# A mixture-of-experts kernel in which the last possible blocks of tokens stand behind a branch on the number of blocks needed

## The chip, the cores and the metric

The kernel runs on one core of a Trainium2 chip. A core has five engines with a queue of instructions each: TensorE (PE, matrix products; its weight loads are listed as PEld), VectorE (DVE), ScalarE (ACT), GpSimd (POOL) and SyncE (SP), and DMA engines that move data between the main memory (HBM) and the core's own memory (SBUF). TensorE writes into banks of a small accumulation memory, from which VectorE and ScalarE read. Engines wait for each other by semaphores. The metric is the time of one execution on the device in microseconds, as a median of several runs.

## The reference

The input is 2048 tokens of 256 numbers. A causal attention with 16 heads is added to it and the sum normed. Then comes the part that the change touches, a mixture of 16 experts of which each token uses two:

```
scores = softmax(t @ gate_w.T);  weights, indices = top_k(scores, 2)
for e in range(16):
    w_e = sum(where(indices == e, weights, 0), axis=-1)
    y = y + swiglu(t, w1[e], w3[e], w2[e]) * w_e[:, None]     # inner width 176
z = swiglu(t, sw1, sw3, sw2)                                  # shared experts, width 352
return layernorm(x + y + z)
```

Here swiglu(t, a, b, o) is (silu(t @ a.T) * (t @ b.T)) @ o.T. Each expert is applied only to the tokens that chose it, which the kernel has to sort out itself.

## The kernel before

**Attention** takes the first part, to about 600 us of the profiled execution. Near its end the gate is computed for each quarter of 512 tokens (`choose`, `settle`), and `scatter` writes each token's row (256 numbers, its number and its first expert) with an indirect DMA into `xg` in HBM, twice, once for each of its two experts. Every expert has room for 2048 rows there; unused rows hold a blank row whose number lies outside the result.

**Blocks.** An expert's rows are worked off in blocks of 128 rows. 4096 rows in all, spread over 16 experts with a partly filled block each, need 47 blocks at most (NBLK = (4096 - 16) // 128 + 16). `table` works out on VectorE, from the experts' counts, the running sum `end` of the experts' blocks, and from it the starting row (`row`) and the expert (`own`) of each block. Blocks beyond the number needed get the blank rows behind the last expert. `keys` gives each block a number by which its rows know whether this is their first or second expert.

**The pipeline of a block b** uses all five engines:
- `load_block`: SP reads `row[b]` into a register and loads 128 rows (129 KB) from `xg` into `xb`. Eight buffers exist, and eight loads (DEPTH + 2) are issued ahead.
- `turn`: TensorE transposes the block (`px`), VectorE copies it to SBUF (`xbT`).
- `hidden`: TensorE reads `own[b]` into a register and multiplies with this expert's w1 and w3 (`ph`); ScalarE takes the Silu (`ru`), VectorE multiplies (`rh`).
- `turn_hidden`: TensorE transposes that (`pT`), ScalarE copies it (`hT`).
- `output`: TensorE multiplies with w2 (`py`), ScalarE copies the result (`yb`), VectorE works out where each row goes (`to`), and GpSimd scatters the rows with an indirect DMA into `yg` in HBM. Rows with a place beyond 4095 are not written.

TensorE's instructions stay in the order in which they are written down: hidden(b), output(b - 1), turn_hidden(b), turn(b + 2). The other engines' orders are made by a scheduler. Banks, `yb`, `to` and `xbT` come from small rings of two or three buffers, so that a step waits until an earlier block has left its buffer.

**Shared experts and the end.** The shared experts' products go through `shared_hidden(c, i)` (`h` on TensorE, `u` on ScalarE, `sh` on VectorE) and `shared_out(c)` (`pz` on TensorE, `z` on VectorE). Those of quarters 3 and 0 and one piece of quarter 1 stand ahead of the blocks; the rest of quarter 1 and quarter 2 stand behind. Then `fetch` loads the two results of each token from `yg` (`got`, eight loads of 512 KB; the first waits until every scatter into `yg` has landed), and `combine` weights and adds them to `z` (VectorE), takes mean and variance (`st`, `m`), a root (`rs`, ScalarE with its own table load) and writes the normed rows `o`, which SP stores.

Of the kernel before, what the change touches and what calls it, by code (L numbers as in the profile page):

```python
# [11 lines left out]
I32 = mybir.dt.int32  # L12
# [5 lines left out]
P = 128  # L18
# [9 lines left out]
NEXP, INTER, SHARED = 16, 176, 352  # L28
# [8 lines left out]
NBLK = (2 * S - NEXP) // P + NEXP  # L37
WARM = 3
LAST = 2
DEPTH = 6  # L40
SCALE = 0.25
EPS = 1e-5
# [4 lines left out]
def block_kernel(  # L47
# [14 lines left out]
    nc = tc.nc  # L62
# [78 lines left out]
    def matmul(*args, **kw):  # L141
        pe(nc.tensor.matmul, *args, **kw)

    def transpose(*args):
        pe(nc.tensor.transpose, *args)
# [31 lines left out]
    def turned(c, bank):  # L177
        for k in range(2):
            pt = bank(f"pt1_{c}_{k}")
            for t in range(4):  # L180
                transpose(pt[:, t * P : (t + 1) * P], xr[c][:, t, k * P : (k + 1) * P], ident)
            nc.vector.tensor_copy(x1T[c][:, k, :], pt)
# [75 lines left out]
    def disjoint(those, group, put):  # L258

        if those:  # L260
            tc.declare_no_dep(put, group=group, reason="no two go to the same rows")
        tc.add_to_no_dep_group(group, put)
        those.append(put)

    def wait_for(those, load):

        for put in those:
            tc.add_manual_dep(
                load.ins, put.name,
                mybir.DependencyInfo(mybir.DependencyClass.Sync, mybir.DependencyReason.DATA),  # L270
                reason="rows of any scatter",
            )
# [12 lines left out]
    with ExitStack() as att:  # L285
# [378 lines left out]
        at = {}  # L664
        chosen = {}

        def put(step, what, *args):
            at.setdefault(step, []).append(lambda: what(*args))
# [23 lines left out]
        for (g, c), i in s_last.items():  # L692
            put(i + (4 if g + 1 < G else 2), finish, g, c)
            if g == G - 1:
                put(i + 2, normed, c)
                if c != LAST:
                    put(i + 6, turned, c, bank)
# [42 lines left out]
    fp1 = ctx.enter_context(tc.tile_pool(name="fp1", bufs=1))  # L740
# [7 lines left out]
    for j in range(2):  # L748
# [5 lines left out]
    blocks = fp1.tile([P, 1], F32, tag="blocks", name="blocks")  # L754
    nc.gpsimd.iota(
        blocks, pattern=[[0, 1]], base=0, channel_multiplier=1,
# [53 lines left out]
    def shared(c):  # L810
        for i in range(NSC):
            shared_hidden(c, i)
        shared_out(c)

    def table():

        count = fp1.tile([P, NEXP], F32, tag="count", name="count")
        nc.vector.tensor_tensor(count, fill, room, ALU.subtract)
        whole = fp1.tile([P, NEXP], I32, tag="whole", name="whole")
        nc.vector.tensor_scalar(whole, count, float(P - 1), None, ALU.add)  # L820
        nc.vector.tensor_scalar(whole, whole, 7, None, ALU.logical_shift_right)
        nb = fp1.tile([P, NEXP], F32, tag="nb", name="nb")
        nc.vector.tensor_copy(nb, whole)
        ends = fp1.tile([P, NEXP, NEXP], F32, tag="ends", name="ends")
        nc.vector.tensor_tensor(
            ends, upto, nb.unsqueeze(1).to_broadcast([P, NEXP, NEXP]), ALU.mult
        )
        end = fp1.tile([P, NEXP], F32, tag="end", name="end")
        nc.vector.tensor_reduce(end, ends, AX.X, ALU.add)

        past = fp1.tile([P, NEXP], F32, tag="past", name="past")
        nc.vector.tensor_scalar(past, end, blocks, None, ALU.is_le)
        owner = fp1.tile([P, 1], F32, tag="owner", name="owner")
        nc.vector.tensor_reduce(owner, past, AX.X, ALU.add)
        nc.vector.tensor_tensor(past, past, nb, ALU.mult)
        first = fp1.tile([P, 1], F32, tag="first", name="first")
        nc.vector.tensor_reduce(first, past, AX.X, ALU.add)
        nc.vector.tensor_tensor(first, blocks, first, ALU.subtract)
        nc.vector.tensor_scalar(
            first, first, float(S // P - 1), float(P), ALU.min, ALU.mult  # L840
        )
        nc.vector.scalar_tensor_tensor(first, owner, float(S), first, ALU.mult, ALU.add)
        row = fp1.tile([P, 1], I32, tag="row", name="row")
        nc.vector.tensor_scalar(row, first, float(NEXP * S), None, ALU.min)
        own = fp1.tile([P, 1], I32, tag="own", name="own")
        nc.vector.tensor_scalar(own, owner, float(NEXP - 1), None, ALU.min)
        return own, row, end

    def keys(end):

# [13 lines left out]
    def load_block(b, row):  # L864
        r = nc.values_load(
            row[b : b + 1, 0:1], engines=[mybir.EngineType.SP],
            min_val=0, max_val=NEXP * S,
            skip_runtime_bounds_check_because="an expert below their number, a block of its room",
        )
        xb[b] = fp8.tile([P, ROW], F32, tag="xb", name=f"xb{b}")  # L870
        load = nc.sync.dma_start(out=xb[b], in_=xg[bass.ds(r, P), :])
        tc.keep_in_program_order(load)
        if b == 0:
            wait_for(scattered, load)

    def turn(b):
        px = ps_a.tile([P, 2, P], F32, tag="t", name=f"px{b}")
        for k in range(2):
            transpose(px[:, k, :], xb[b][:, k * P : (k + 1) * P], ident)
        xbT[b] = fp3.tile([P, 2, P], F32, tag="xbT", name=f"xbT{b}")  # L880
        nc.vector.tensor_copy(xbT[b], px)  # L881

    def hidden(b, own):
        expert[b] = nc.values_load(
            own[b : b + 1, 0:1], engines=[mybir.EngineType.PE], min_val=0, max_val=NEXP - 1,
            skip_runtime_bounds_check_because="a count of experts, held below their number",
        )
        ph = ps_a.tile([P, 2 * INTER], F32, tag="h", name=f"ph{b}")
        for k in range(2):
            matmul(  # L890
                ph, lhsT=xbT[b][:, k, :],
                rhs=w13[:, k].rearrange("p n f -> p (n f)")[
                    :, bass.ds(expert[b] * (2 * INTER), 2 * INTER)
                ],
                start=(k == 0), stop=(k == 1),
            )
        u = fp2.tile([P, INTER], F32, tag="ru", name=f"ru{b}")
        nc.scalar.activation(u, ph[:, :INTER], AF.Silu)  # L898
        us[b] = fp2.tile([P, INTER], F32, tag="rh", name=f"rh{b}")
        nc.vector.tensor_tensor(us[b], u, ph[:, INTER:], ALU.mult)  # L900

    def turn_hidden(b):
        pT = ps_a.tile([P, 2, P], F32, tag="t", name=f"pT{b}")
        for k in range(2):
            transpose(pT[:HK, k, :], us[b][:, k * HK : (k + 1) * HK], ident)
        hT[b] = fp3.tile([HK, 2, P], F32, tag="hT", name=f"hT{b}")
        nc.scalar.copy(hT[b], pT[:HK])  # L907
# [3 lines left out]
    def output(b, key):  # L911
        py = ps_a.tile([P, E], F32, tag="y", name=f"py{b}")
        for k in range(2):
            matmul(
                py, lhsT=hT[b][:, k, :],
                rhs=w2r[:, k].rearrange("p n e -> p (n e)")[:, bass.ds(expert[b] * E, E)],
                start=(k == 0), stop=(k == 1),
            )
        yb = fp3.tile([P, E], F32, tag="yb", name=f"yb{b}")
        nc.scalar.copy(yb, py)  # L920
        to = fp3.tile([P, 1], I32, tag="to", name=f"to{b}")
        nc.vector.scalar_tensor_tensor(  # L922
            to, xb[b][:, E + 1 : ROW], key[:, b : b + 1], xb[b][:, E : E + 1],
            ALU.not_equal, ALU.add,
        )
        disjoint(
            back, "back",
            nc.gpsimd.indirect_dma_start(  # L928
                out=yg[:, :], out_offset=bass.IndirectOffsetOnAxis(ap=to[:, 0:1], axis=0),
                in_=yb, in_offset=None, bounds_check=2 * S - 1, oob_is_err=False,  # L930
            ).ins,
        )
# [41 lines left out]
    shared_hidden(3, 1)  # L974
    turned(LAST, spare)
    shared_hidden(3, 2)
    both = choose(LAST, spare)
    shared_out(3)
    shared_hidden(0, 0)
    settle(LAST, spare, both)  # L980
    for t in range(4):
        scatter(LAST, t)
    own, row, end = table()
    for b in range(DEPTH + 2):
        load_block(b, row)
    key = keys(end)
# [1 line left out]
    shared_hidden(0, 2)  # L988
    shared_out(0)
    shared_hidden(1, 0)  # L990
    turn(0)
    turn(1)
    for b in range(NBLK):
        hidden(b, own)
        if b > 0:
            output(b - 1, key)
        turn_hidden(b)
        if b + 2 < NBLK:
            turn(b + 2)
        if b + DEPTH + 2 < NBLK:  # L1000
            load_block(b + DEPTH + 2, row)
    output(NBLK - 1, key)
    shared_hidden(1, 1)
    shared_hidden(1, 2)
    shared_out(1)
    shared(LAST)
    fetched = {}
# [72 lines left out]
```

## Time and profile before

| what | value |
|---|---|
| median of 3 runs | 818.64 us (816.54 to 819.76) |
| the profiled execution, its time | 821.03 us |
| the profiled execution, its span | 819.3 us |
| busy: PE, PEld, DVE, ACT, POOL | 790.6, 371.8, 552.0, 452.9, 328.0 us |
| first load of a block issued | 637.0 us |
| last product of a block on TensorE starts | 777.74 us |
| last instruction of ScalarE's normed rows starts | 814.95 us |

The span reaches from the first to the last instruction; the time of an execution also holds what lies around it. A row of the timeline gives the start in microseconds, the duration, the engine, the line, the operation with the tiles that it writes and reads, how often it stands there, and in brackets the idle time ahead of it with the engine that ended it. All matmuls have line L139, a helper's, so they are told apart by their tiles. A row of the table by stretches gives the stretch, its length, the busy time of PE, PEld, DVE, ACT and POOL with the number of their instructions, TensorE's granted clock, the DMA engines' busy share and GB/s. In the chain that ended last each row is what the next one waited for.

### The profile page before, as it was taken

The page shows a single profiled execution, that of the slowest core. Times are in us where ns is not written, and L with a number is a line of the kernel's source. Part 1 is how long each engine was busy: PE and PEld are TensorE (multiplying, and loading weights), DVE is VectorE, ACT ScalarE, POOL GpSimd, SP SyncE. Part 2 cuts the span into 40 slices and gives each one's busy share as a digit, 9 for nine tenths or more (in the row PEclk, how much of TensorE's full clock was granted, in tenths as well). Part 3 has the DMA queues.
Part 4 walks back from the last instruction along what each step waited for, and adds up shares of the span by engine and source line. Part 5 has one row for each costly group of instructions (what it writes and reads, how often), then busy time and mean ns, then how long its engine had stood idle before and what let it go on. Part 6 is the DMA issues. An engine that isn't in the chain of part 4 may idle for free. (4 is left out here: it accounts for less than half of the span.)

```text
span 819.3 us, 15191 instructions
## 1 busy us (share of the span) xinstructions
PE 790.6 (96%) x5146; PEld 371.8 (45%) x5146; DVE 552.0 (67%) x1503; ACT 452.9 (55%) x1014; POOL 328.0 (40%) x562
## 2 busy tenths in 40 slices
PE   7999999999999999999999999999999899999994
PEld 3444433534333344534344444443356466666652
DVE  2769888986777887787887777887466233333266
ACT  1143556387776886676786668756531233333346
POOL 2042535344454554455354546433553133333300
PEclk9999999999999999999999999999899999999998
DMA  5479999960000000010000000001152322222062
GB/s 145 130 190 334 325 331 325 318 191 2 1 1 2 1 1 2 1 36 18 2 1 1 2 1 1 2 1 53 52 161 78 98 84 86 83 79 76 16 206 102
DMA packets 68339, 72.56 MB, mean 89 GB/s; under 512 B 5056, under 2 KB 62499, under 8 KB 68262
## 3 DMA queue, kind: packets, MB, share of 16 engines
q1 hardware_dynamic: 63006, 62.43, 26.3%
q0 software_dynamic: 3792, 8.43, 2.9%
q10 hardware_dynamic: 1464, 0.72, 0.4%
q8 instruction: 42, 0.69, 0.3%
q14 instruction: 35, 0.29, 0.1%
HBM read 27.10 MB, written 46.43 MB: 90 GB/s over the span
## 5 line engine op out<-in xcount | busy, mean ns | idle before, releaser
L534 ACT ACTIVATE p<-s 128x512 f32<-128x512 f32 (+3 forms) x640 | 292.7, 540 | 131.6 <-PE m L139 77.5
L139 PE MATMUL m<-k,q 32*128 32x512 f32 (+3 forms) x1280 | 303.3, 564 | 0.8 <-DVE rot L422 0.5
L139 PE MATMUL s<-qa,k 32*128 32x512 f32 (+3 forms) x1280 | 280.4, 558 | 3.3 <-DVE avs L562 2.3
L489 DVE TENSOR_REDUCE pm<-m 128x1 f32<-128x512 f32 x384 | 237.5, 681 | 44.0 <-PE m L139 43.6
L566 POOL TENSOR_TENSOR avs<-avs,more 128x512 f32<-128x512 f32 (+3 forms) x125 | 136.8, 1094 | 166.4 <-ACT more L565 162.8
L139 PEld LDWEIGHTS s<-qa,k 32*128 32x128 f32 x1280 | 107.3, 184 | 120.3 <-ACT p L534 67.4
L139 PE MATMUL av<-p,v 128*32 128x512 f32 (+3 forms) x1280 | 156.6, 546 | 0.9 <-ACT p L534 0.4
L139 PEld LDWEIGHTS m<-k,q 32*128 32x128 f32 x1280 | 122.8, 183 | 44.4 <-issue 12.0
L484 DVE CUSTOM_DVE_ANT_0 m<-m,qmask 128x512 f32<-128x512 f32 (+3 forms) x256 | 118.2, 521 | 28.8 <-PE m L139 25.8
L565 ACT COPY more<-av 128x512 f32<-128x512 f32 (+3 forms) x125 | 65.6, 525 | 38.3 <-PE av L139 31.4
L928 POOL DMA_INDIRECT yg<-yb,to x47 | 46.3, 985 | 99.1 <-DVE to L922 51.0
L538 POOL TENSOR_SCALAR_AFFINE_SELECT p<-p 128x128 f32<-128x128 f32 x256 | 70.6, 297 | 38.2 <-ACT p L534 36.4
L139 PEld LDWEIGHTS av<-p,v 128*32 128x32 f32 x1280 | 27.3, 108 | 104.5 <-ACT p L534 53.6
L139 PE MATMUL ph<-w,xbT 128*128 x188 | 68.8, 490 | 2.3 <-DVE xbT L881 1.7
L900 DVE TENSOR_TENSOR rh<-ru,ph 128x176 f32<-128x176 f32 x47 | 15.9, 337 | 61.9 <-ACT ru L898 61.9
L898 ACT ACTIVATE ru<-ph 128x176 f32<-128x176 f32 x47 | 14.9, 318 | 66.9 <-PE ph L139 65.6
L139 PE MATMUL py<-w2r,hT 88*128 x188 | 48.5, 380 | 0.5 <-ACT hT L907 0.5
L139 PE MATMUL h<-xT,cs 128*128 128x512 f32 (+1 forms) x96 | 43.3, 597 | 2.4 <-ACT u L791 1.4
L277 POOL DMA_INDIRECT xg<-xr,slot x32 | 31.1, 972 | 32.6 <-issue 21.3
L139 PEld LDWEIGHTS ph<-w,xbT 128*128 128x128 f32 x188 | 32.4, 191 | 23.2 <-issue 13.4
L139 PEld LDWEIGHTS py<-w2r,hT 88*128 88x128 f32 x188 | 35.5, 189 | 13.3 <-ACT hT L907 1.1
L427 POOL TENSOR_TENSOR k<-rot 128x512 f32<-128x512 f32 x16 | 20.3, 1268 | 42.6 <-DVE rot L425 42.6
(146 smaller groups left out, 649.0 us busy)
## 6 DMA issues: line engine op xcount, KB each, us to landing
xg<-hot SPq DMA_DIRECT2D x16, 2064.0 KB
xb<-xg SPq DMA_DIRECT2D x47, 129.0 KB
w<-in_w_dram SPq DMA_DIRECT2D x4, 1408.0 KB
got<-yg SPq DMA_DIRECT2D x8, 512.0 KB
w2r<-in_w_dram SPq DMA_DIRECT2D x2, 1408.0 KB
xr<-in_x_dram SPq DMA_DIRECT2D x4, 512.0 KB
out_dram<-o SPq DMA_DIRECT2D x8, 256.0 KB
cs<-in_rope_dram SPq DMA_DIRECT2D x16, 80.0 KB
```

Of the source, the lines that this page charges most:

```text
L139: tc.keep_in_program_order(op(*args, **kw))
L277: put = nc.gpsimd.indirect_dma_start(out=xg[:, :], out_offset=bass.IndirectOffsetOnAxis(ap=slot[:, j, i : i + 1], axis=0), in_=xr[c][:, t, ...
L427: nc.gpsimd.tensor_tensor(ks[g, c], tmp[:, 0, :], tmp[:, 1, :], ALU.add)
L484: nc.vector.tensor_tensor_reduce(out=ps[:, :n], in0=ps[:, :n], in1=qmask[:, CH - n :], scale=1.0, scalar=3.0 * NEG, op0=ALU.add, op1=ALU.m ...
L489: nc.vector.tensor_reduce(to, ps, AX.X, ALU.max)
L534: nc.scalar.activation(pr[:, n0:], ps[:, n0:], AF.Exp, scale=SCALE)
L538: nc.gpsimd.affine_select(out=diag, in_=diag, pattern=[[1, P]], base=0, channel_multiplier=-1, compare_op=ALU.is_ge, fill=0.0,)
L565: nc.scalar.copy(more[:, n0:], pv[:, n0:])
L566: nc.gpsimd.tensor_tensor(to, to, more[:, n0:], ALU.add)
L898: nc.scalar.activation(u, ph[:, :INTER], AF.Silu)
L900: nc.vector.tensor_tensor(us[b], u, ph[:, INTER:], ALU.mult)
L928: nc.gpsimd.indirect_dma_start(out=yg[:, :], out_offset=bass.IndirectOffsetOnAxis(ap=to[:, 0:1], axis=0), in_=yb, in_offset=None, bounds_c ...
```

## The change

The loop over the blocks becomes a function `in_turn(first, last)` that starts and ends its own pipeline. It is called for blocks 0 to 41. Then the number of blocks that the routing needs, the last entry of `end`, which `table` now also returns as an integer in a tile of its own, is read into a register on every engine, and a branch follows: if it is over 42 (OFTEN), the five remaining blocks are loaded and worked off by a second `in_turn`; if not, none of their instructions is executed. The shared experts and the end stand behind the branch.

```
+OFTEN = 42
 def table():
...
+        total = fp1.tile([P, 1], I32, tag="total", name="total")
+        nc.vector.tensor_copy(total, end[:, NEXP - 1 :])
-        return own, row, end
+        return own, row, end, total
...
-    turn(0)
-    turn(1)
-    for b in range(NBLK):
-        hidden(b, own)
-        if b > 0:
-            output(b - 1, key)
-        turn_hidden(b)
-        if b + 2 < NBLK:
-            turn(b + 2)
-        if b + DEPTH + 2 < NBLK:
-            load_block(b + DEPTH + 2, row)
-    output(NBLK - 1, key)
+    def in_turn(first, last):
+
+        turn(first)
+        turn(first + 1)
+        for b in range(first, last):
+            hidden(b, own)
+            if b > first:
+                output(b - 1, key)
+            turn_hidden(b)
+            if b + 2 < last:
+                turn(b + 2)
+            if b + DEPTH + 2 < last:
+                load_block(b + DEPTH + 2, row)
+        output(last - 1, key)
+
+    in_turn(0, OFTEN)
+    blocks_in_all = nc.values_load(
+        total[0:1, 0:1], min_val=0, max_val=NBLK,
+        skip_runtime_bounds_check_because="the sum of the experts' blocks, NBLK at most",
+    )
+    with tc.If(blocks_in_all > OFTEN):
+        for b in range(OFTEN, NBLK):
+            load_block(b, row)
+        in_turn(OFTEN, NBLK)
     shared_hidden(1, 1)
     shared_hidden(1, 2)
     shared_out(1)
```

More of the change, by code (lines that the diff above doesn't have):

```diff
@@ L982, in block_kernel @@
         scatter(LAST, t)
-    own, row, end = table()
+    own, row, end, total = table()
     for b in range(DEPTH + 2):
```

## The prediction, made before the result was known

> **What bounds the kernel now.** I read the busy table by stretches first, then TensorE's timeline around the last blocks, then the chain that ended last, then DMA traffic block by block. One execution was profiled: 821.03 us, span 819.3, so 1.7 lie around the span; it stands 2.4 above the median of 818.64. A saving is the same number of microseconds in both, so I subtract from the median.
>
> Busy time by stretch (us; busy by engine with instruction counts; clock; DMA share; GB/s):
> ```profile
> 650.00:720.00 70.00, 69.62 (x295) 44.65 (x293) 22.97 (x74) 24.89 (x74) 23.64 (x24) 1.00 0.28 84
> 764.40:778.71 14.31, 13.76 (x59) 8.80 (x58) 3.84 (x12) 5.10 (x15) 4.95 (x6) 1.00 0.02 5
> 778.71:819.30 40.59, 28.76 (x89) 15.74 (x87) 26.39 (x89) 22.76 (x37) 0.98 (x1) 0.94 0.48 156
> ```
> In the block stage TensorE (first number) is busy 69.62 of 70.00; the others idle half the time or more. What takes a block off TensorE takes it off the span.
>
> ```profile
> 743.21 1.45 PE L139 MATMUL ph<-w,xbT 128*128 x4
> 744.49 1.03 PE L139 MATMUL py<-w2r,hT 88*128 x4
> 745.44 0.42 PE L139 MATMUL pT<-ident,rh 128*88 128x128 f32 x2
> 745.69 0.38 PE L139 MATMUL px<-ident,xb 128*128 128x128 f32 x2
> 746.07 1.45 PE L139 MATMUL ph<-w,xbT 128*128 x4
> ...
> 777.74 1.13 PE L139 MATMUL py<-w2r,hT 88*128 x4 [0.46 <-ACT hT L907]
> 778.71 7.03 PE L139 MATMUL h<-xT,cs 128*128 128x512 f32 x16
> 785.57 1.03 PE L139 MATMUL pz<-cs,sh 128*128 128x256 f32 x4
> 787.56 2.65 PE L139 MATMUL pz<-cs,sh 96*128 96x256 f32 x11 [0.96 <-DVE sh L793]
> ```
> The reader sees one block per 746.07 - 743.21 = 2.86 us (2.864 over several), no gaps, and then the shared experts' matmuls following the last block's `py` at once.
>
> The chain at that seam:
> ```profile
> 779.60 2.10 DMA yg<-yb,to
> ...
> 781.90 3.71 DMA got<-yg
> ...
> 785.63 0.55 DVE z L950 x2
> ...
> 786.91 0.60 DVE sh L793
> ...
> 787.56 4.61 PE pz L139 x20
> ```
> So two things leave the block stage: TensorE's line of work, and the last scatter of rows, its landing at 781.70, the first gather `got` (3.71 us) and VectorE's combining. They meet again at `pz` at 787.56, where TensorE waits 0.96 for `sh`.
>
> **Is the branch skipped?** The traffic of single blocks says so:
> ```profile
> 760.50:763.40 2.90, 2.90 (x13) 1.88 (x13) 1.00 (x4) 1.04 (x4) 0.98 (x1) 1.00 0.13 45
> 763.40:766.30 2.90, 2.90 (x13) 1.88 (x14) 1.02 (x4) 1.06 (x4) 0.98 (x1) 1.00 0.05 17
> 766.30:769.10 2.80, 2.79 (x13) 1.77 (x13) 0.92 (x4) 0.96 (x4) 0.98 (x1) 1.00 0.01 0
> ```
> The scatter that starts at 779.60 is block 46's (counted from 0); counting back, 763.44 is block 40's and 766.30 block 41's. Block 40 moves 17 GB/s x 2.9 us = 49 KB, some 48 rows of 1 KB; from block 41 on nothing is written. So 41 blocks carry rows, and 41 is not over 42: the branch leaves out blocks 42 to 46, and block 41 is still computed for nothing.
>
> **What is removed.** Five blocks of TensorE time: 5 x 2.864 = 14.32 us. With them go five loads of 129 KB, five scatters and the blocks' steps on VectorE and ScalarE (3.84 and 5.10 us in the stretch of 14.31 above), all beside TensorE, worth nothing more. The first part now ends as the whole ends today (block 41 has no later block to transpose, as 46 has none now), so its drain (0.46 before the last `py`) stays the same.
>
> **What is added ahead of the branch.** One copy `total` on VectorE: near 0.12 us (`own`, also one column to int32, takes 0.147) in the table of blocks. It delays `row` to about 630.3; the first load of a block starts only at 637.0, because it waits for the last scatters. Covered by 6.7 us; without that cover it would cost 0.12.
>
> **The branch.** Each engine reads `total` into a register, compares, jumps over the body to a short alternative that waits for this engine's own earlier work and adds to its semaphores what the body would have added, then goes on. The trace has no branch. Register reads it has: 0.275 us on SP's queue (`row`), 0.307 on TensorE's (`own`). ScalarE, VectorE and GpSimd also step over five semaphore waits first, all satisfied long ago, 0.02 to 0.05 each. Per engine I take 0.15 + 0.3 + 0.1 for the jump = 0.55, bounds 0.3 to 2.7 (a jump that must fetch its target, taken as the smallest transfer of this trace, 2.1 us from issue to landing). A gain from the jump itself is excluded: nothing runs sooner.
>
> [...] The row:
> ```profile
> q8 instruction: 42, 0.69, 0.3%
> ```
> 10292 matmul and weight-load records are about 245 for each of these 42 packets of 16.4 KB, which I therefore take for TensorE's. [...] I take no fetch. [...]
>
> Who is queued behind: on TensorE the shared experts' `h` now waits for ScalarE to have finished `yb` of the last block and passed the branch, since its bank's semaphore count includes the skipped body. I write all times on the clock of before (really 14.32 earlier). `yb` runs 778.95 to 779.32; ScalarE is through at about 779.6, and `h` starts at 779.65 rather than 778.71: 0.94 later. On SP, the loads are long issued, so it passes the branch early and stands at `got` as before. GpSimd passes the branch after dispatching its last scatter at 779.36, done by 780.0 to 780.6, before that scatter lands at 781.70, so `got` still lands at 785.63. VectorE passes early too.
>
> **What is moved.** The branch is a border for the scheduler, and behind it VectorE's order differs: the first `z` (needs `got`) now stands ahead of `sh` (1,1), and ten pieces of combining (six `z`, two `st`, two `m`) ahead of `sh` (1,2), where three stood. ScalarE does two roots per table load, so 5 table loads replace 7. Walking through it, with the spacing of the same rows in the timeline (z 0.39, sh 0.60, st 0.33, m 0.09):
> - `sh`(1,1): 785.63 + 0.40 = 786.03 to 786.71 (before, 782.41). TensorE's fourth `h` reuses its bank and must wait: 786.76 to 788.45. (TensorE alone would have been there at 784.85, so the 0.94 above is hidden, with 1.9 of slack for a slower branch.)
> - `sh`(1,2): its place in VectorE's queue is 785.63 + 0.40 + 0.60 + five z, two st, two m = 1.95 + 0.66 + 0.18 = 789.4, ends 790.05. `pz` resumes at 790.1, against 787.56: 2.55 late.
> - h(2,0) 794.55; its Silu ends 798.25; h(2,1) at 798.45 against 795.90: still 2.55.
> - Between them ScalarE no longer has the two `o` (1.08) in the way, but one more root (0.25): h(2,2) at 802.05 against 800.39: 1.65 late.
> - The last `sh` needs its Silu by 804.7 and its bank by 805.45: TensorE no longer waits 0.67 for it. Last `pz` ends 0.8 later than before, and the tail of VectorE and ScalarE (DVE `z`, `st`, ACT `o`) follows as before: 0.8 late.
>
> Bounds for this reorder: 0 (all reabsorbed in the tail), 2.55 (nothing reabsorbed); below nothing only by the two saved table loads, 2 x 1.28, if ScalarE set the end; it doesn't in the walk. I take 0.8, and 0.3 for the hand-overs of a semaphore that I didn't count.
>
> **Sum:** -14.32 + 0.8 + 0.3 = -13.2. On the profile's own 821.03: 807.8. On the median: 818.64 - 13.2 = 805.4.
>
> **Rivals.**
> - *GpSimd holds up the gather* (0.16). The trace has a drain on GpSimd's queue that starts at 779.4 behind the last scatter and lasts 7.745 us, to 787.1, though the scatter landed at 781.70. If GpSimd's part of the alternative (it adds to the scatters' semaphores, on which `got` waits) must wait for the same thing, `got` starts 5.4 later. For it: that drain. Against it: scatters follow each other at 1.97, and the same kind of semaphore instruction took 27 ns at the kernel's start. Time: 805.4 + 5.4 = 810.8.
> - *Fetch stalls* (0.10): one or two engines in series at 2.1, less the slack of 1.9 on TensorE and ScalarE but without slack on GpSimd: 806 to 809.6.
> - *The branch costs most of the blocks* (0.04): drain, stalls and reorder add up to 10 to 17: 809 to 818 with most near 815, no change by this measurement. Nothing in the trace has that size.
> - *The branch is taken* (0.03), slower: the change then doesn't do what it says, and five blocks are done in a second, separate pipeline. Its place is the seam at block 42, it decides from a need of 43 blocks on. Price: the first part drains (the last block today takes 778.71 - 774.64 = 4.07 for 2.86, 1.2), the second fills (first `px` 639.10 to first `ph` 642.21 is 3.1, of which about 1.3 is VectorE's other work, so 1.0 to 2.3 beyond the transposes' own 0.76; and 6.17 for the first two blocks instead of 5.73), 0.8 for the reorder and 0.3 to 0.55 for the branch: 3.9 to 5.3, say 4.3, and 823.0. Against it: the 0 GB/s from block 41 on.
>
> **How the numbers follow.** Forecast 0.67 at 805.4, its own range 803 to 807.5 (reorder 0 to 2.55; runs differ by up to 0.25%). The range reaches up to 811.5 to take in the gather held up. Half a per cent is about what a measurement of this kernel can tell from no change: 814.5 to 822.7. Faster: 0.67 + 0.16 + 0.10 = 0.93; same 0.04; slower 0.03.
>
> **What would show it.** Right: TensorE has 42 `ph` groups at 2.86; `h` starts 1.9 us or so after the last `py` starts (0.97 now); `got` starts 2.3 after the last scatter's start; `sh`(1,1) comes after the first `z`; TensorE idles some 1.9 ahead of the fourth `h` and 0.7 ahead of `pz`. Wrong: 47 groups; `got` starting 7 us after the last scatter; GpSimd or ScalarE idle for over 2 us with nothing named; new instruction packets at the seam.

## The result, and the profile after

| what | before | after |
|---|---|---|
| median | 817.59 us (4 runs, 815.56 to 819.76) | 804.96 us (4 runs, 803.10 to 808.38) |
| profiled execution, its span | 819.3 us | 801.1 us |
| from the start of the last block's `py` to the end of the span | 819.3 - 777.74 = 41.56 us | 801.1 - 757.86 = 43.24 us |

The change saves 12.6 us; the ratio is 0.985 (95% interval 0.9804 to 0.9896). The forecast was -13.2 and 805.4. On another chip, side by side with two other kernels, the same two gave 818.18 and 805.32, ratio 0.9851 (0.9832 to 0.987).

The two profiled spans differ by 18.2 us, which is not what the change is worth. Some 5.6 of it lies ahead of the last block beyond the five blocks themselves: 777.74 - 757.86 = 19.88, less 14.32. The granted clock fell in before's profile (0.83 in the stretches from 560 to 580 and from 640 to 650 us) where after's shows 1.00. So the single profiles are read here from one event to the next inside a stage, and medians are kept for the total. Executions disturbed as a whole are left out of every comparison.

First the number of blocks. This is the row of the page of after for the scatters (line, engine, operation, tiles, count, busy and mean), and the row of its DMA queues for instruction packets, of which the page of before counts 42:

```profile
L931 POOL DMA_INDIRECT yg<-yb,to x42 | 41.4, 985 | 88.2 <-ACT yb L923 44.1
...
q8 instruction: 41, 0.67, 0.4%
```

There are 42 scatters and not 47, so the five blocks were skipped. The number of instruction packets, 41 for 42, doesn't tell what the jump did. Their times say more, and come with the branch's own rows below.

The stretches of after: the block stage, the 2.40 us in which the last `py` runs and the branch is passed, and the whole tail from the last `py` on.

```profile
650.00:720.00 70.00, 69.57 (x294) 44.60 (x293) 22.93 (x73) 24.80 (x74) 23.63 (x24) 1.00 0.28 84
757.86:760.26 2.40, 1.13 (x4) 0.68 (x4) 0.00 (x0) 0.37 (x1) 1.42 (x2) 1.00 0.09 27
757.86:801.10 43.24, 30.21 (x92) 16.45 (x92) 26.59 (x89) 20.21 (x35) 1.87 (x2) 0.95 0.45 147
```

The block stage is as it was, with TensorE (first number) busy 69.57 of 70.00. In the 2.40 us of the seam TensorE works only 1.13: a gap that was not there. TensorE's timeline in the tail of after shows what follows from it:

```profile
757.86 1.13 PE L140 MATMUL py<-w2r,hT 88*128 x4 [0.46 <-ACT hT L910]
760.26 5.42 PE L140 MATMUL h<-xT,cs 128*128 128x512 f32 x12 [1.27 <-ACTq L1014]
767.68 1.96 PE L140 MATMUL h<-xT,cs 128*96 128x512 f32 x4 [2.00 <-DVE sh L794]
769.47 1.03 PE L140 MATMUL pz<-cs,sh 128*128 128x256 f32 x4
771.04 4.60 PE L140 MATMUL pz<-cs,sh 96*128 96x256 f32 x20 [0.54 <-DVE sh L794]
775.47 3.60 PE L140 MATMUL h<-xT,cs 128*128 128x512 f32 x8
779.38 7.38 PE L140 MATMUL h<-xT,cs 128*128 128x512 f32 x16 [0.31 <-ACT u L792]
786.59 5.60 PE L140 MATMUL pz<-cs,sh 128*128 128x256 f32 x24
```

There are three idle times where before had one: 1.27 ahead of `h`, ended by ScalarE's queue at line 1014 (the branch); 2.00 ahead of the fourth `h`, ended by VectorE's `sh`; 0.54 ahead of `pz`. In return two later ones are gone: `h` from 779.38 on runs 16 matmuls on end, and the last 24 `pz` have no break.

Three rows of before for the same part, from `h`(2,1) on, where it waits for ScalarE's `u` and VectorE's `sh`:

```profile
795.90 3.70 PE L139 MATMUL h<-xT,cs 128*128 128x512 f32 x8 [0.31 <-ACT u L791]
800.39 3.67 PE L139 MATMUL h<-xT,cs 128*96 128x512 f32 x8 [0.79 <-ACT u L791]
...
805.60 4.60 PE L139 MATMUL pz<-cs,sh 96*128 96x256 f32 x20 [0.67 <-DVE sh L793]
```

The chain that ended last, after (start, duration, what):

```profile
749.29 13.15 DMA yg<-yb,to
...
762.72 3.79 DMA got<-yg
...
766.54 0.03 DVE z L953
...
766.95 0.68 DVE sh L794
...
770.41 0.58 DVE sh L794
...
771.04 4.60 PE pz L140 x20
```

The gather `got` leads to the first `z`, this now to `sh`, and a row of combining separates this `sh` from the next one at 770.41, which TensorE's `pz` waits for. Before, the first of the two started at 782.41, ahead of the gather's first `z` at 785.63.

The times of the tail, counted from the start of the last `py` (777.74 before, 757.86 after):

| event | before | after | later by | forecast |
|---|---|---|---|---|
| first `h` starts | 0.97 | 2.40 | 1.43 | 0.94 |
| first gather `got` starts | 4.16 | 4.86 | 0.70 | 0 |
| `pz` resumes | 9.82 | 13.18 | 3.36 | 2.55 |
| h(2,1) starts | 18.16 | 21.52 | 3.36 | 2.55 |
| h(2,2) starts | 22.65 | 25.22 | 2.57 | 1.65 |
| last `pz` ends | 32.46 | 34.33 | 1.87 | 0.8 |
| end of the span | 41.56 | 43.24 | 1.68 | 1.1 |

(777.74 + 9.82 = 787.56 is the `pz` of before, 757.86 + 13.18 = 771.04 that of after, and so on.) Five blocks less at 2.864 and 1.68 more in the tail are -14.32 + 1.68 = -12.64, against -12.6 measured in medians; the interval of the medians, 8.5 to 16.0 us saved, is much wider than the difference.

Last, the branch itself, which the profile before could not show. Rows of after by source line: register read of `total`, then compare-and-branch and what stands in the short alternative (engine's queue, operation, count, ns min/median/max, first and last start in us):

```profile
L1010 SPq TENSOR_LOAD <-total x1: 270/270/270, 732.3 to 732.3; - x1
L1010 DVEq TENSOR_LOAD <-total x1: 543/543/543, 757.1 to 757.1; - x1
L1010 PEldq TENSOR_LOAD <-total x1: 303/303/303, 758.0 to 758.0; - x1
L1010 ACTq TENSOR_LOAD <-total x1: 478/478/478, 759.5 to 759.5; - x1
L1010 POOLq TENSOR_LOAD <-total x1: 500/500/500, 759.9 to 759.9; - x1
```
```profile
L1014 SPq COMPARE_BRANCH  x1: 50/50/50, 732.6 to 732.6; - x1
L1014 DVEq COMPARE_BRANCH  x1: 72/72/72, 757.7 to 757.7; - x1
L1014 PEldq COMPARE_BRANCH  x1: 364/364/364, 758.4 to 758.4; - x1
L1014 ACTq COMPARE_BRANCH  x1: 54/54/54, 760.0 to 760.0; - x1
L1014 POOLq COMPARE_BRANCH  x1: 45/45/45, 760.5 to 760.5; - x1
L1014 POOLq INC_SWDGE_SEM  x1: 1666/1666/1666, 760.8 to 760.8; - x1
```

SP, VectorE and TensorE pass early. ScalarE reads at 759.5, when its last `yb` is done, and gets through at 760.2, and only then may `h` start at 760.26. GpSimd is last: it reads at 759.9, and its semaphore instruction runs from 760.8 to about 762.5; `got` starts at 762.72.

No engine stands long at the jump: each queue's next instruction stands 0.1 to 0.5 us behind the start of its branch, or 0.6 on TensorE (759.0), whose branch itself takes 0.36. A packet of 16 KB of instructions does start at 759.54, 1.14 us after TensorE's branch and 15.4 us after the packet before it (744.10), where those of the block stage are 22 to 26 us apart. That the jump brought it forward is the author's reading of these times. It takes 1.2 us, and `h` starts at 760.26, before it has landed, so `h` didn't wait for it.

### The profile page after: what moved, and what is told of

Read it like the earlier page. It is cut to its first block, busy times and chain, and to the rows that moved or that the text cites. A ratio compares the mean times of both kernels' runs of the same rounds, so it can differ in the third digit from the quotient of the medians.

```text
span 801.1 us, 14999 instructions
## 1 busy us (share of the span) xinstructions
PE 771.5 (96%) x5086; PEld 361.3 (45%) x5086; DVE 547.1 (68%) x1489; ACT 445.0 (56%) x997; POOL 323.0 (40%) x557
## 5 line engine op out<-in xcount | busy, mean ns | idle before, releaser
L140 PE MATMUL av<-p,v 128*32 128x512 f32 (+3 forms) x1280 | 154.2, 540 | 1.9 <-DVE base L244 1.2
L931 POOL DMA_INDIRECT yg<-yb,to x42 | 41.4, 985 | 88.2 <-ACT yb L923 44.1
L140 PE MATMUL ph<-w,xbT 128*128 x168 | 60.3, 482 | 2.4 <-DVE xbT L884 1.7
L903 DVE TENSOR_TENSOR rh<-ru,ph 128x176 f32<-128x176 f32 x42 | 14.2, 338 | 53.7 <-ACT ru L901 53.7
L140 PE MATMUL py<-w2r,hT 88*128 x168 | 43.4, 380 | 0.7 <-ACT hT L910 0.7
L140 PEld LDWEIGHTS ph<-w,xbT 128*128 128x128 f32 x168 | 28.5, 189 | 20.8 <-issue 11.6
L140 PEld LDWEIGHTS py<-w2r,hT 88*128 88x128 f32 x168 | 31.7, 189 | 12.0 <-ACT hT L910 1.2
```

Source lines behind the costliest of these rows:

```text
L140: tc.keep_in_program_order(op(*args, **kw))
L931: nc.gpsimd.indirect_dma_start(out=yg[:, :], out_offset=bass.IndirectOffsetOnAxis(ap=to[:, 0:1], axis=0), in_=yb, in_offset=None, bounds_c ...
```

## The experiments

Diffs are against the changed kernel unless they say otherwise. The theory at the start: the saving is TensorE's time for five blocks (14.3), and something under 2 us is given back at the border, part by the branch itself and part by VectorE's order behind it. Rivals: the skipped blocks are worth less than 14.3 and the branch costs nothing; or the branch costs more and hides a larger saving. The tails of all kernels are compared in one table at the end of this section.

**No branch at all.** 42 blocks and nothing behind them, so what a routing with over 42 blocks would need is left out.

```
     in_turn(0, OFTEN)
-    blocks_in_all = nc.values_load(total[0:1, 0:1], ...)
-    with tc.If(blocks_in_all > OFTEN):
-        ...
     shared_hidden(1, 1)
```

> Blocks 42 to 46 are left out of the program altogether, with no branch (valid only for a routing that needs 42 blocks at most). Theory: five blocks are worth 5 x 2.864 = 14.3 us of TensorE, and the branch with the border that it puts into the scheduler's order gives 1.7 of it back. Then this kernel is 14.3 below before, and from the start of the last py to the end of the span it takes 41.6 as before (43.24 with the branch). Rival: five blocks are worth only 12.6, since something beside TensorE holds the end, and the branch is free: 12.6 below before.

Measured: 811.05 us on a chip on which the kernel before takes 825.23; 14.18 less, ratio 0.984 (0.9818 to 0.9862). TensorE's timeline of this kernel at the seam:

```profile
767.76 1.13 PE L140 MATMUL py<-w2r,hT 88*128 x4 [0.46 <-ACT hT L910]
768.73 7.03 PE L140 MATMUL h<-xT,cs 128*128 128x512 f32 x16
...
777.68 4.60 PE L140 MATMUL pz<-cs,sh 96*128 96x256 f32 x20 [1.06 <-DVE sh L794]
```

`h` follows `py` at 0.97 and `pz` resumes at 9.92, as before the change (0.97 and 9.82), and the tail is 41.54 for 41.56. The interval of the medians, 11.4 to 15.0 us, doesn't exclude the rival's 12.6; the tail does. So the blocks are worth 14.3 and leave no price of their own: the tail's 1.7 belongs to the branch and its border.

**The border without the saving.** All 47 blocks, then the branch's code with a condition that no routing meets.

```
-    in_turn(0, OFTEN)
+    in_turn(0, NBLK)
...
-    with tc.If(blocks_in_all > OFTEN):
+    with tc.If(blocks_in_all > NBLK):
```

> All 47 blocks are computed ahead of the branch, and the branch (never taken, over 47 blocks needed, same body) follows: the branch's price alone. Theory: 1.7 above before, and 43.2 from the start of the last py to the end. Rival (the branch is free, the blocks are worth less): as before, 41.6.

Measured: 826.88 us (22 runs) against 825.23 (27 runs), 1.65 slower, ratio 1.0021 (1.001 to 1.0032). With the kernel above, -14.18 + 1.65 = -12.5, for the -12.6 of the whole change. TensorE's timeline of this kernel:

```profile
782.73 5.39 PE L140 MATMUL h<-xT,cs 128*128 128x512 f32 x12 [0.60 <-ACTq L1014]
790.12 1.96 PE L140 MATMUL h<-xT,cs 128*96 128x512 f32 x4 [2.01 <-DVE sh L794]
...
793.60 4.60 PE L140 MATMUL pz<-cs,sh 96*128 96x256 f32 x20 [0.66 <-DVE sh L794]
```

Its last `py` starts at 781.00. The profile shows less than a branch that is not taken: it has no register read of `total` and no compare-and-branch, on any engine, where the changed kernel has five of each. `total` is declared to be NBLK at most, so a condition of over NBLK was probably settled when the program was built; that is not shown. What is left is the border: the alternative's waits and semaphores on every engine, and the order that the scheduler makes behind them.

So the run gives the border's price without that of the branch's own instructions. ScalarE signals at 782.6, right behind its last `yb`, and `h` starts at 1.73 and not 2.40. GpSimd's semaphore instruction starts at 782.8 and takes 1.78, but beside the last scatter (782.85), not behind it: `got` starts at 785.17, which is 4.17, as in the kernel before. Still the fourth `h` waits 2.01 for `sh`, and the tail is 823.9 - 781.00 = 42.90. Most of the price, 42.90 - 41.54 = 1.36, is thus there with no branch executed and a gather that isn't late. The reads, compares and jumps of the changed kernel, with the gather that they delay, add 43.24 - 42.90 = 0.34; that is one profile against one, though a second profile of the changed kernel has 43.25.

**VectorE's order behind the branch.** To see whether the order is that price, VectorE is made to take `sh`(1,1) ahead of the gather's first `z`, and `sh`(1,2) no later than two `z` behind it. Nothing else is changed by hand, though with this order ScalarE has two table loads more.

```
+        gated[c, i] = nc.vector.tensor_tensor(hs[c, i][:m, :], u[:m, :], pss[1][:m, :], ALU.mult).ins
...
+                if h == 6 or (h in (7, 0) and j == 0):
+                    wait_for([gated[1, 1 + (h != 6 or j)]], weighted)
```

> The changed kernel, with VectorE made to take sh(1,1) ahead of the first piece of combining, and sh(1,2) after two of them. Theory: most of the 1.7 is VectorE's order behind the branch: TensorE no longer waits 2.0 ahead of the fourth h, pz resumes about 10.3 after the start of the last py (9.82 before, 13.18 in the changed kernel), and the end comes 42.0 to 42.6 after it: about 1 below the changed kernel. Rival: the price is the jump and the semaphores themselves (h 1.4 late, gather 0.7 late), order is harmless: 43.2 stays.

Measured: 813.66 us, 11.57 under the kernel before, ratio 0.985 (0.9831 to 0.987); no gain by the median over what the whole change gives. Its profile doesn't say why, because the granted clock fell just at the seam. A stretch of this kernel:

```profile
770.00:780.00 10.00, 9.28 (x19) 4.09 (x20) 1.91 (x4) 2.47 (x3) 0.98 (x1) 0.83 0.54 197
```

At 0.83 the 16 `h` took 8.83 us for the 7.13 that a second profile of the same kernel shows.

> The same kernel as x3_gates_first, whose profile fell into a dip of TensorE's clock at the seam (weight loads 0.85 apart there instead of 0.43), for a profile without one. Theory (VectorE's order is most of the price): pz starts 9.3 after the start of the last py and isn't held up for more than 0.3, and the end comes 42.1 to 42.8 after it. Rival: pz is early, but ScalarE's seven table loads instead of five and VectorE's later pieces give it back: 43.2 or more.

Measured: 805.19 us (one run) on a chip with 817.82 before. Its last `py` starts at 760.33, and TensorE's timeline goes on:

```profile
762.72 7.13 PE L140 MATMUL h<-xT,cs 128*128 128x512 f32 x16 [1.26 <-ACTq L1016]
769.69 5.71 PE L140 MATMUL pz<-cs,sh 128*128 128x256 f32 x24
775.23 3.60 PE L140 MATMUL h<-xT,cs 128*128 128x512 f32 x8
```

The waits of 2.00 and 0.54 for `sh` are gone, `pz` runs 24 matmuls on end, and h(2,0) starts at 14.90 and not 17.61 (775.47 - 757.86). But at the end of the span the tail is 802.6 - 760.33 = 42.27, only 0.97 under the changed kernel: of the 2.7 us that TensorE gained, 1.7 are lost again. TensorE loses 1.1 of it, where it waits for ScalarE's `u` twice (0.38 and 0.31, once in the changed kernel) and for `sh` again (0.67); the rest goes behind the last `pz`, from which it is 9.57 to the end for 8.91. What ScalarE's two further table loads have to do with that was not tried apart. So this order, with them, is worth 1.0 of the tail's 1.7, and with the better order 42.27 - 41.54 = 0.73 is left for the late `h` and the late gather. The medians (-11.57, and -12.6 for one run) do not resolve a size of 1 us; this split rests on the profiles.

**One piece of the shared experts ahead of the branch.** Work for TensorE while the others pass the branch:

```
     in_turn(0, OFTEN)
+    shared_hidden(1, 1)
     blocks_in_all = nc.values_load(
...
-    shared_hidden(1, 1)
     shared_hidden(1, 2)
```

> The changed kernel with shared_hidden(1,1) moved ahead of the branch: TensorE has 3.4 us of work while ScalarE and VectorE finish the last block and cross the branch, and sh(1,1) stands ahead of the border. Theory: h(1,2) starts without the 1.3 idle, no 2.0 ahead of the fourth h, pz resumes 9.8 to 10.3 after the start of the last py, end at 41.8 to 42.6. Rival (GpSimd's late gather carries the price): VectorE's combining still starts 0.8 late, and the end stays at 43.0 or more.

Measured: 806.26 us, ratio 0.9865 (0.9837 to 0.9892), 11.6 less than before. In its profile `h`(1,1) follows `py` at 0.97 again, but `h`(1,2) waits 1.62 for VectorE's queue at the branch, since VectorE now comes there behind `sh`(1,1), which ends at 763.67; it branches at 764.1. The tail is 801.0 - 758.31 = 42.69, 0.55 less than the changed kernel's, and the gather starts at 4.86, as late as there. Neither the theory's 41.8 to 42.6 nor the rival's 43.0 came true: part of the wait is gone, and most has only moved to another engine.

**The branch where the engines wait anyway.** The five rare blocks, behind their branch, come first; then the loads and the 42 blocks. Ahead of the first block TensorE waits: in the kernel before its last `h` ends at 638.25, and the first `px` starts at 639.10, behind the first load of a block, which is issued at 637.01, when the last scatters into `xg` have landed.

```
-        if b == 0:
+        if b in (0, OFTEN):
             wait_for(scattered, load)
...
-    for b in range(DEPTH + 2):
-        load_block(b, row)
...
-    in_turn(0, OFTEN)
     blocks_in_all = nc.values_load(
...
         in_turn(OFTEN, NBLK)
+    for b in range(DEPTH + 2):
+        load_block(b, row)
+    in_turn(0, OFTEN)
     shared_hidden(1, 1)
```

> The branch with the five rare blocks stands ahead of the other 42, where every engine waits for the last scatters into xg anyway, so there is no border at the end. Theory: the jump and GpSimd's 1.67 us semaphore instruction are hidden there; 41.6 from the start of the last py to the end, and 14.3 below before; up to 1 more if VectorE's older work clears ahead of the first blocks. Rival (the branch has its price wherever it stands): 12.6 below before, with the 1.7 now lost ahead of the first block.

Measured: 810.17 us, 15.06 under the kernel before and 0.88 under the one without a branch, ratio 0.9824 (0.9806 to 0.9843). Rows of this kernel at the branch's line, and TensorE's timeline at the first transposes and at `pz`:

```profile
L1011 POOLq INC_SWDGE_SEM  x1: 828/828/828, 636.9 to 636.9; - x1
L1011 PEldq COMPARE_BRANCH  x1: 362/362/362, 637.3 to 637.3; - x1
L1011 DVEq COMPARE_BRANCH  x1: 72/72/72, 642.9 to 642.9; - x1
```
```profile
643.37 0.93 PE L140 MATMUL px<-ident,xb 128*128 128x128 f32 x4 [1.73 <-DVEq L1011]
...
775.42 4.60 PE L140 MATMUL pz<-cs,sh 96*128 96x256 f32 x20 [0.94 <-DVE sh L794]
```

The first `px` waits for VectorE's branch, but the first `ph` does not come later for it. Counted from the first `h` of the shared experts near 600 us it starts at 645.38 - 602.93 = 42.45, and without a branch, on the same chip, at 645.98 - 603.24 = 42.74. The tail is 807.1 - 765.62 = 41.48, and `pz` resumes at 9.80. In this profile the border's price is gone and has not come back where the branch now stands.

**The branch taken.** OFTEN is 40, and 41 blocks are needed, so the five (here seven) rare blocks are worked off.

```
-OFTEN = 42
+OFTEN = 40
```

> OFTEN is 40, so that with 41 blocks needed the branch is taken and blocks 40 to 46 run in the second pipeline: the rival on the slower side, tried. By its price: TensorE drains (1.2), the second pipeline fills (1.4 to 2.8), the tail's border costs 1.7 where it is crossed, so 3.5 to 5.5 above before, near 830 on a chip where before takes 825. The other theory (an engine can run ahead through the branch, the loads of SP above all): about 2 above before.

Measured: 821.3 us against 817.82, 3.5 slower, ratio 1.0046 (1.0031 to 1.0062). TensorE's timeline at the seam of this kernel:

```profile
754.12 1.13 PE L140 MATMUL py<-w2r,hT 88*128 x4 [0.46 <-ACT hT L910]
755.08 0.60 PE L140 MATMUL px<-ident,xb 128*128 128x128 f32 x4
755.99 2.63 PE L140 MATMUL ph<-w,xbT 128*128 x8 [0.30 <-DVE xbT L884]
759.00 0.42 PE L140 MATMUL pT<-ident,rh 128*88 128x128 f32 x2 [0.39 <-DVE rh L903]
...
761.29 1.35 PE L140 MATMUL ph<-w,xbT 128*128 x4
```

From the `py` of block 39 to the `ph` of block 42 it takes 761.29 - 754.12 = 7.17. In the unbroken pipeline this is two blocks less the 1.28 from a `ph` to the `py` behind it, 2 x 2.864 - 1.28 = 4.45; so the seam costs 2.7. The tail is 819.4 - 775.71 = 43.69, 2.13 over before's, of which 1.47 is one row: four `h` that took 3.43 (from 784.93 on) for 1.96 in the changed kernel. By an estimate that is a fall of the granted clock, as above where 16 `h` took 8.83 for 7.13 at 0.83. Without it the two are 2.7 + 0.7 = 3.4, for 3.5 in the medians.

**One block fewer ahead.** The early branch with 41 blocks, all of which carry rows.

```
-OFTEN = 42
+OFTEN = 41
```

> x4_branch_early with OFTEN 41, the number that this routing needs: block 41 is left out too. Theory (TensorE's 2.864 for each block, whatever it holds): 2.9 below x4_branch_early, that is 17.9 below before. Rival (an empty block is cheaper than its turn on TensorE, since it moves no rows): under 2 below x4_branch_early.

Measured: 802.41 us against 817.82, 15.4 less, ratio 0.9829 (0.9801 to 0.9857); 2.5 short of what was expected, with runs from 798.98 to 806.58. Its profile has one block fewer and a tail of 797.3 - 755.52 = 41.78, so by the events inside it the block's 2.86 and the border's 1.5 are both saved.

**The three side by side.** To settle that, the changed kernel and the two with an early branch ran on one chip, five runs each.

> The changed kernel as it stands, next to two others on one chip. Theory (five blocks at 2.864 less, 1.7 given back at the border): 12.6 us under the kernel before. Rival (the tail differs from run to run and the two measurements so far agreed by chance): anything from 10 to 16 under it.

> The branch with its five blocks ahead of the first load of a block. Theory: the whole price of the border goes, so 1.7 us less than the changed kernel on the same chip, 14.3 under the kernel before, and a tail of 41.5 us from the last py on. Rival (only the border in the tail goes, and its price comes back where the branch now stands, ahead of the first blocks): no difference to the changed kernel, with the first block's ph about 1.5 later after the shared experts' last h than there.

> The early branch with one block fewer ahead of it (41 and not 42). Theory: one block more is skipped, 2.86 us less than the kernel with the early branch at 42, 17.2 under the kernel before. Rival (the last block that carries rows is now followed at once by the gather, whose scatter of 17 GB/s lands later than an empty one's): only 1 to 2 us less.

Measured, with 818.18 before: 805.32 (ratio 0.9851, 0.9832 to 0.987) as changed; 805.1 (0.9842, 0.9826 to 0.9858) with the early branch; 804.63 (0.9823, 0.9801 to 0.9845) with the early branch at 41. For the changed kernel the theory holds (-12.9). For the other two the medians fall short of it: 0.2 instead of 1.7, and 0.5 instead of 2.86 beyond that. The profiles say where it went. The early kernel's tail is 804.7 - 763.20 = 41.50, and its first `ph` starts 42.55 after the first shared `h`, against 42.93 in the changed kernel: both as expected. But then the first two blocks' `ph` run at a lower granted clock. First, the stretch from 640 to 650 us of the changed kernel on this chip; second, that of the early one (granted clock is the third number from the end); third, a row of the early one's timeline:

```profile
640.00:650.00 10.00, 9.76 (x44) 6.53 (x43) 2.72 (x9) 3.25 (x10) 1.99 (x2) 1.00 0.42 119
```
```profile
640.00:650.00 10.00, 9.25 (x29) 5.90 (x29) 2.56 (x8) 1.96 (x6) 1.00 (x1) 0.71 0.37 105
```
```profile
640.51 5.06 PE L140 MATMUL ph<-w,xbT 128*128 x8 [0.90 <-DVE xbT L884]
```

Eight `ph` take 5.06 for 2.60 in the changed kernel, and from the first `ph` to the last `py` it is 122.69 for 119.31, 3.4 us more for the same 42 blocks. The mean granted clocks of the five runs were 0.986, 0.985 and 0.982. Single runs at equal clock have the expected order: at 0.990 the spans are 802.1 as changed and 798.8 with the early branch at 41. The early kernel at 41 blocks has the same fall here (0.66 from 640 to 650 us). Whether an early branch brings it about is open, but it is not peculiar to one: the fall stands in two of the four profiles with an early branch (not in the early kernel's first one, nor in that at 41 blocks on another chip) and in four of the nine others, those of before, of the kernel without a branch, of the border alone and of the first with `sh` moved ahead.

An estimate from these events makes the early branch at 41 blocks the better kernel, by 43.24 - 41.78 + 2.86 = 4.3 us. No side-by-side median shows that: by medians it was ahead of the changed kernel by 0.7 on this chip, with intervals that overlap.

The tails from the start of the last `py` on, in us, with what is left of the border's price:

| kernel | first `h` | `got` | `pz` resumes | end of span | over no branch |
|---|---|---|---|---|---|
| before | 0.97 | 4.16 | 9.82 | 41.56 | 0.0 |
| 42 blocks, no branch | 0.97 | 4.06 | 9.92 | 41.54 | |
| 47 blocks, border without branch instructions | 1.73 | 4.17 | 12.60 | 42.90 | 1.4 |
| as changed | 2.40 | 4.86 | 13.18 | 43.24 | 1.7 |
| as changed, on another chip | 2.39 | 4.85 | 13.13 | 43.25 | 1.7 |
| VectorE's `sh` first | 2.39 | 4.85 | without a break | 42.27 | 0.7 |
| one piece ahead | 0.97 | 4.86 | without a break | 42.69 | 1.2 |
| early branch | 0.97 | 4.06 | 9.80 | 41.48 | -0.1 |

## Why the prediction was right, and where its terms were off

The forecast of 805.4 came true at 804.96, and -13.2 at -12.6, by the mechanism that it gave. That the two agree to 0.6 us is closer than the medians can tell; the terms below are judged by the events in the profiles.

- **The blocks, -14.32.** Right: removed alone they gave -14.18, and they leave the tail as it was (41.54 for 41.56).
- **Whether the branch is skipped.** Right: 42 scatters. The evidence, no bytes written from block 41 on, was confirmed from the other side: with a border at 40 the branch is taken, with one at 41 it is not.
- **No fetch at the jump.** Right in that no engine waited for one. Its sign of being wrong, a new packet of instructions at the seam, did appear, at 759.54, but TensorE's queue had gone on at 759.0. That there would be no fetch to wait for was the author's estimate, which nothing in the profile before showed; in the trace of the change the next instruction stands 0.1 to 0.6 us behind the start of each branch. No run shows the 0.1 for compare-and-branch either: it took 45 to 72 ns on four engines and 364 on TensorE.
- **The branch per engine, 0.55.** A little low where it mattered. ScalarE was put at through with the branch 0.28 after `yb` (779.6 less 779.32); it took about 0.75 (759.45 to 760.2). That is five waits, a register read of 0.48 for the assumed 0.3, and the alternative behind the jump. `h` came 1.43 late for 0.94. As the prediction said, this is hidden by the later wait for `sh`: the fourth `h` waited 2.00, for 1.9 forecast.
- **GpSimd and the gather, 0.** This term was mis-sized. The prediction let GpSimd be done with the branch before the last scatter lands, from a semaphore instruction of 27 ns. The one that really stands there took 1.67 us (1.78 and 0.83 in other kernels), behind a register read of 0.5. It ended at about 762.5, and the landing, by an estimate, at 759.72 + 2.10 = 761.82, with the 2.10 of before's last scatter. So `got` came 0.70 late. It is the first rival's mechanism at an eighth of its size (5.4): GpSimd does hold up the gather, but by one slow instruction, and not by the drain of 7.7 us that the rival rested on (6.11 us here, from 762.5 on, while `got` starts at 762.72).
- **The reorder, +0.8.** The walk through it was right in its places: the fourth `h`, `pz` 2.55 late, h(2,1), the vanished 0.67 ahead of the last `pz`. All are there, each later than forecast by 0.8 to 1.1. The border alone, with the gather on time, shows how much of that is the walk's own: against before, `pz` and h(2,1) are 2.78 late for 2.55 each, the last `pz` ends 1.29 late for 0.8, and the span 1.34 for 1.1 (the 0.8 and the 0.3 for hand-overs). So the start of the walk was right to 0.2, and at its end it took too much for reabsorbed.
- **Sum of the tail.** +1.68 for the 1.1 forecast. Of the 0.6 between them, 0.24 is the border's (1.34 for 1.1), and 0.34 the branch's own instructions with the late gather, put at nothing there.
- **The rival of the branch taken.** It did not happen with 42, but its price was measured: 3.5 for the 4.3 given, and under the 3.9 to 5.3 around it (its parts add up to 3.7 at the low end, not 3.9). The seam cost 2.7, near the low end of its three parts for the drain and the fill, 1.2 + 1.0 + 0.44.

## What to carry to other kernels

Blocks that carried no rows were worth TensorE's full time for them, in a stage that kept it busy for 69.62 of 70.00 us: without them the kernel took 14.18 us less, for 5 x 2.864 = 14.32. The branch's own instructions, with the gather that they delay, cost 0.34; the larger part of its price, 1.36 of 1.7 here, came from the border: with the border alone `h` waited 0.60 there for ScalarE, and behind it, in VectorE's new order, TensorE waited 2.01 and 0.66 for `sh`. So a place for it is where the engines wait for something else anyway: in the profiles that took the tail from 43.24 back to 41.48, though side by side the medians differed by only 0.2 us. Read a saving of this size from one event to the next within a stage, with the granted clock beside it, before reading it from two spans.

## What was not expected of the hardware

- Reading one number, `total`, into a register took 270 ns on SP, 303 on TensorE, 478 on ScalarE, 500 on GpSimd and 543 on VectorE.
- Compare-and-branch over the five blocks took 362 to 379 ns on TensorE, but 45 to 72 on the other four engines. Where the blocks were worked off, TensorE's two rows of it took 90 and 189 ns.
- In the changed kernel's profile a packet of instructions started 1.14 us after TensorE's branch and 15.4 after the one before, where 22 to 26 lay between those of the block stage; `h` started ahead of its landing.
- GpSimd's semaphore instruction in the short alternative, INC_SWDGE_SEM, took 1666 ns in the changed kernel (it ended at 762.47, and `got` started at 762.72), 1778 with the border alone and 828 with an early branch. What sets its length is open; in the shortest case its engine stood ahead of the blocks and not behind a scatter of results.
- The three chips differ in the same kernel before by more than half of what the change is worth: 825.23, 817.82 and 818.18 us. Where the granted clock falls for some 10 us, as in the profile with 0.71 from 640 to 650 us, 3.4 us are lost, twice the price of the branch.
